# A third query product by an inner Strassen scheme in 128 columns, in a multi-query attention layer

## The chip, the cores and the metric

The kernel runs on one core of a Trainium2 chip. The engines of the core are TensorE (PE, with its weight loads listed apart as PEld), VectorE (DVE), ScalarE (ACT), GpSimd (POOL) and SyncE (SP, which issues the transfers here). The metric is the time of one execution on the device in microseconds; the kernel before takes 1023.08 us, the median of three runs.

## The reference

For each of 64 batches of 128 tokens the layer is attention with 16 query heads and a single key and value head, with a bias, a mask, a null key and a residual:

```python
xn = layernorm(x, g_in)
q = (xn @ Wq).reshape(b, n, H, DH).transpose(0, 2, 1, 3) * scale
kv = xn @ Wkv
k, v = (kv[..., :DH], kv[..., DH:])
...
sim = jnp.einsum('bhid,bjd->bhij', q, k)
...
attn = jax.nn.softmax(sim, axis=-1)
out = jnp.einsum('bhij,bjd->bhid', attn, v)
out = out.transpose(0, 2, 1, 3).reshape(b, n, INNER)
out = out @ Wo
return layernorm(out, g_out)
```

The model width is 512, the inner width 1024 (16 heads of 64), everything in float32. The result is added to x.

## The kernel before, in words

Batches are taken in groups of four (g) for the query product and in pairs (d) for everything else; one pass over a pair is a `turn(d)` (scores and attention times values) followed by a `body(d)` (all else). There is no scheduler: each engine has one queue, and the order in it is the order in which the source lines issue the work. A body of pair d makes, side by side, the key and value product of the next group (`kv_pair`), half of the next group's queries, the softmax of the pair, and the output projection and the norm of the pairs before it.

The query product of a group and the output projection of a pair are each done by Strassen's scheme: seven products of half-size blocks instead of eight. In this text "query product k" is `product(g, f, k)` and "output product k" is `out_product(p, k)`, k from 1 to 7. A query product is made for one chunk f of 128 query columns at a time, with 256 tokens as the moving columns: two matmuls of 128x128 weights and 256 columns, one for each half of the contraction. Each body does two chunks, f0 and f1. An output product is four matmuls of 256 columns.

In the bodies with d > 3 (d = 4 to 29, named `deeper` in the code) query products 2 and 4 are not made as a whole. They are split by Strassen's scheme a second time, into seven single matmuls of 128 columns for both chunks together: `inner_product` and `last_product`. "Inner product k.i" is the i-th of these within query product k. The same scheme is not used there for query product 3.

Partial sums of a scheme accumulate in a PSUM bank, are read out by ScalarE or VectorE, and are accumulated further by the next product: query products 1, 6, 7 of a chunk in bank `a` (`keep` copies the stages p1, u2, u3 to tiles of their own in SBUF), 5 and 3 in bank `c`; output products 1, 6, 7, 4 in bank `X`, 5 and 3 in `Y`. So a product that goes on in a bank must wait until the stage before it has been read. `q_out`, `inner_out`, `last_out` and `out_part` add what stands in PSUM to a kept stage on VectorE. The inner products of query product 4 use the two banks of pool `ps_s`, those of query product 2 one of the two banks of `ps_w`.

On VectorE the same queue holds `scores_max`, `rinv` (reciprocal of the softmax sum), `blocks_T` (a transpose of a batch's whole attention matrix, 128x1536) and the norms' statistics; on POOL it holds `scale` (softmax times the reciprocal), `bias_add`, the token sums of the schemes and the power -0.5 of the norms; ScalarE has the exponentials, the copies of PSUM and the applied norms.

## Time and profile before

| | |
|---|---|
| Time, median of three runs | 1023.08 us (1022.87 to 1023.58) |
| Span of the profiled execution | 1021.2 us |
| Time around the span (median less span) | 1.9 us |
| PE busy | 1012.8 us, 99% |
| PEld busy | 899.6 us, 88% |
| DVE busy | 845.8 us, 83% |
| POOL busy | 769.2 us, 75% |
| ACT busy | 673.1 us, 66% |

Busy time of an engine is the time in which at least one of its instructions is under way. Each float32 matmul of the program is two records in the trace, so one 128x256 matmul is two records of 128x256. The duration in a group of matmuls is that of one record from its start until its result is written; records overlap, so the time that a row of matmuls takes on PE is read from the start of one group to the start of the next. Line numbers are those of the kernel before.

### The profile page before, as it was taken

To read this page: it belongs to the slowest core of one execution; us is meant where nothing else is said; L and a number is where in the kernel's file an instruction comes from. 1 tells how busy PE (TensorE), PEld (TensorE's weight loads), DVE (VectorE), ACT (ScalarE), POOL (GpSimd) and SP (SyncE) were. 2 spreads that over 40 slices of the span, in tenths; PEclk is the share of its full clock that TensorE was granted. 3 is DMA by queue.
4 is the path that set the end of the run, shared out by engine and by line. 5 is a ranking of instruction groups with operands and counts; after the bars stand their busy time and mean duration, and the time that the engine had idled before them with its cause. 6 is when DMAs were issued, how large, how long until landed. Compare 5 with 4: busy or idle time off the path is not lost.

```text
span 1021.2 us, 31459 instructions
## 1 busy us (share of the span) xinstructions
PE 1012.8 (99%) x12333; PEld 899.6 (88%) x12333; DVE 845.8 (83%) x1958; ACT 673.1 (66%) x2753; POOL 769.2 (75%) x633
## 2 busy tenths in 40 slices
PE   9999999999999999999999999999999999999997
PEld 8888888888888888888888888888888888888886
DVE  6777888888888888888888888888898888977787
ACT  5766677656677665686656776566775657865583
POOL 4997768677686877859678696776868768686686
PEclk9999999999999999999999999999999999999999
DMA  7415143151531415225152341514315152140221
GB/s 219 139 30 151 67 122 112 36 154 63 144 98 69 123 56 152 88 74 140 36 152 85 109 120 32 164 63 138 102 50 134 64 152 89 71 111 24 69 85 62
DMA packets 73835, 100.86 MB, mean 99 GB/s; under 512 B 32212, under 2 KB 36056, under 8 KB 71896
## 3 DMA queue, kind: packets, MB, share of 16 engines
q1 hardware_dynamic: 73392, 98.47, 32.5%
q8 instruction: 96, 1.57, 0.6%
q14 instruction: 51, 0.42, 0.1%
q10 hardware_dynamic: 296, 0.40, 0.1%
HBM read 63.19 MB, written 33.55 MB: 95 GB/s over the span
## 4 chain that ended last, share of the span: by engine, by line
PE 96%; POOL 1%; DVE 1%; ACT 1%; issue 0%; DMA 0%; POOLq 0%; DVEq 0%; ACTq 0%
PE pyX L936 20%; PE pa L515 16%; PE pyY L936 10%; PE pc L515 10%; PE po L849 8%; PE pkv L363 6%; PE pyw L936 5%; PE pl L581 4%; PE pm L647 4%; PE ps L718 3%; PE pq L450 3%; PE sc_X L718 2%; PE sc_Y L718 2%; PE sc_a L718 1%; PE py_s L936 1%; ACT s L749 1%
## 5 line engine op out<-in xcount | busy, mean ns | idle before, releaser
L749 ACT ACTIVATE s<-s,nmax 128x65 f32<-128x65 f32 (+1 forms) x1024 | 372.2, 369 | 61.7 <-DVE nmax L740 61.7
L771 POOL TENSOR_TENSOR s<-s,rinv 128x512 f32<-128x512 f32 (+1 forms) x132 | 190.6, 1446 | 133.1 <-DVE rinv L767 133.1
L683 POOL TENSOR_TENSOR s<-biasp,mneg 128x1552 f32<-128x1552 f32 (+1 forms) x65 | 206.2, 3176 | 50.9 <-DVE s L733 26.9
L749 ACT ACTIVATION_READ_ACCUMULATOR s<-s,nmax 128x1 f32 x1024 | 197.1, 192 | 0.0
L787 DVE STREAM_TRANSPOSE sb<-s 128x1536 f32<-128x1536 f32 (+1 forms) x68 | 113.6, 1674 | 11.4 <-POOL s L771 11.4
L740 DVE TENSOR_REDUCE nmax<-s 128x8 f32<-128x1032 f32 (+1 forms) x128 | 121.8, 952 | 0.1
L964 ACT COPY y<-pyX 128x256 f32<-128x256 f32 x29 | 10.8, 372 | 167.5 <-PE pyX L936 129.7
L936 PE MATMUL pyX<-wT,oT 128*128 128x256 f32 x464 | 109.7, 379 | 0.0
L936 PE MATMUL pyX<-wo,oT 128*128 128x256 f32 x464 | 109.7, 379 | 0.0
L936 PEld LDWEIGHTS pyX<-wo,oT 128*128 128x128 f32 x464 | 86.0, 190 | 10.5
L936 PEld LDWEIGHTS pyX<-wT,oT 128*128 128x128 f32 x464 | 84.0, 190 | 9.2
L916 POOL TENSOR_TENSOR oT<-oT 128x512 f32<-128x512 f32 x64 | 80.6, 1277 | 3.9 <-PE pyw L936 1.6
L849 PE MATMUL po<-sb,vr 32*64 32x128 f32 (+1 forms) x3904 | 82.9, 308 | 0.2 <-DVE sb L787 0.2
L527 ACT COPY ku<-pa 128x256 f32<-128x256 f32 x118 | 43.4, 367 | 59.8 <-issue 30.8
L849 PEld LDWEIGHTS po<-sb,vr 32*64 32x64 f32 x3904 | 71.7, 130 | 9.4 <-issue 5.6
L536 DVE TENSOR_TENSOR qT<-pc,ku 128x256 f32<-128x256 f32 x118 | 48.2, 408 | 32.2 <-PE pc L515 19.7
L868 ACT ACTIVATE oT<-po,nv 128x512 f32<-128x512 f32 (+1 forms) x127 | 73.5, 655 | 0.4 <-PE po L849 0.2
L515 PE MATMUL pa<-xS,wq 128*128 128x256 f32 x264 | 67.8, 379 | 0.0
L597 DVE TENSOR_TENSOR qT<-pl,kp 128x128 f32<-128x128 f32 x112 | 32.1, 286 | 42.8 <-PE pl L581 41.9
L281 POOL TENSOR_TENSOR rstd<-rstd,nhalf 128x1 f32<-128x1 f32 x64 | 35.2, 557 | 42.0 <-DVE rstd L280 38.9
L363 PE MATMUL pkv<-xT,wkv 128*128 128x256 f32 x256 | 63.3, 391 | 0.0
L515 PE MATMUL pa<-xT,wq 128*128 128x256 f32 x236 | 60.6, 379 | 0.0
(207 smaller groups left out, 2588.9 us busy)
## 6 DMA issues: line engine op xcount, KB each, us to landing
res<-in_x_dram SPq DMA_DIRECT2D x64, 256.0 KB
out_dram<-y SPq DMA_DIRECT2D x63, 256.0 KB
x<-in_x_dram SPq DMA_DIRECT2D x62, 256.0 KB
xd<-xb SPq DMA_DIRECT2D x14, 1024.0 KB
xT<-xd SPq DMA_DIRECT2D x56, 256.0 KB
vr<-vd SPq DMA_DIRECT2D x64, 128.0 KB
kT<-kT SPq DMA_DIRECT2D x32, 64.0 KB
vd<-vb SPq DMA_DIRECT2D x32, 64.0 KB
```

The costliest lines, as they stand in the source:

```text
L363: nc.tensor.matmul(pkv, wkv[:, kc, :], xT[g][:, t : t + 2, kc, :], start=(kc == 0), stop=(kc == KC - 1),)
L515: nc.tensor.matmul(prod[tag], w[:, kc, f * P : (f + 1) * P], t[:, :, kc, :], start=(start and kc == 0), stop=(kc == HK - 1), skip_group_ch ...
L683: nc.gpsimd.tensor_tensor(S[b][:, :, keys], biasp[:, :, keys], mneg[:, t, keys] .unsqueeze(1) .broadcast_to([P, R8, keys.stop - keys.start ...
L718: nc.tensor.matmul(home[r][u * DH : (u + 1) * DH, f, :], qT[g, f, t // 2][rows, t % 2, hf, u], kT[rows, 0 : nk // Q, t, :], start=True, st ...
L740: nc.vector.tensor_reduce(nmax[b][:, hf], S[b][:, :, WITH_NULL[hf]], AX.X, ALU.max, negate=True)
L749: nc.scalar.activation(row, row, AF.Exp, bias=nmax[b][:, hf, k : k + 1], accum_out=rsum[b][:, hf, k : k + 1],)
L771: nc.gpsimd.tensor_tensor(sv, sv, rinvs[b, hf][:, lo:hi].unsqueeze(2).broadcast_to([P, hi - lo, sv.shape[2]]), ALU.mult,)
L787: nc.vector.transpose(sbs[b][:, :, lo:hi].rearrange("p j e q -> p e j q"), S[b][:, lo:hi, 1 : ROW - 1].rearrange("p e (j k) -> p e j k", k=Q),
L849: nc.tensor.matmul(po[s][rows, to : to + n], vr[g][quad, t, PLACE[j], :], sb[quad, slots, r * NF : (r + 1) * NF, :], start=(turn == 0), st ...
L868: nc.scalar.activation(to, src, AF.Identity, bias=nv2)
L916: eng.tensor_tensor(o, a, b, op)
L936: nc.tensor.matmul(prod[key], h[:, c, :], w[:, c, :], start=(start and c == 0), stop=(c == HC - 1), skip_group_check=not start,)
```

## The change

**Query product 3** of the bodies with d > 3 is made by the second scheme as well: seven matmuls of 128 columns for both chunks (`inner_products(3, ...)`) take the place of two products of two 256-column matmuls each. Inner products 3.2, 3.3 and 3.4 accumulate into bank `c` on top of query product 5; 3.1, 3.5, 3.6 and 3.7 go to one of the two banks of `ps_s`, whose other bank holds the inner products of query product 4. Both banks are one tile, `pi34`.

**Both chunks' chain in one bank.** `product_two` makes query products 1, 6, 7 and 5 for f0 and f1 one after the other into the two halves of a bank, `keep_two` and `q_out_two` read both halves with one instruction of 512 columns.

**Partial sums** are no longer kept in tiles of their own, but in the query and output tiles in which the result will stand (`KEPT`, `Y_KEPT`).

**Norms in pairs.** `two_stats` and `two_nmr` do the small operations of a norm for two batches with one instruction each; the statistics of the output norm stand at the start of a body instead of one half at the end of the body before.

**The bodies** with d > 3 are a new function, `body_full`, with an order of its own.

```diff
+    def two_stats(tiles, name):
+        mv = small.tile([P, 2, 2], FP, tag=f"mv{name}", name=f"mv{name}")
+        rstd = small.tile([P, 2], FP, tag=f"rs{name}", name=f"rs{name}")
+        sts = []
+        for t in tiles:
+            st = small.tile([P, 6], FP, tag="st", name="st")
+            nc.vector.bn_stats(st, t)
+            sts.append(st)
+        for i, st in enumerate(sts):
+            nc.vector.bn_aggr(mv[:, i], st)
+        nc.vector.tensor_scalar(rstd, mv[:, :, 1], EPS, None, ALU.add)
+        nc.gpsimd.tensor_tensor(rstd, rstd, nhalf.broadcast_to([P, 2]), ALU.pow)
+        return mv, rstd
+    def two_nmr(mv, rstd, name):
+        nmr = small.tile([P, 2], FP, tag=f"nm{name}", name=f"nm{name}")
+        nc.vector.scalar_tensor_tensor(
+            nmr, mv[:, :, 0], -1.0, rstd, ALU.mult, ALU.mult
+        )
+        return [(nmr[:, i : i + 1], rstd[:, i : i + 1]) for i in range(2)]
...
-    def keep(tag, name, slot=None):
...
+    KEPT = {"p1": (0, 0), "u2": (0, 1), "u3": (HC, 0)}
+    def keep(tag, g, f, name):
+        u, h = KEPT[name]
+        nc.scalar.copy(
+            q_part(g, u + f, h), prod[tag].rearrange("p (t h i) -> p t h i", t=2, h=2)
+        )
...
+    def product_two(g, j, k, pool, tag, start=True):
+        if start:
...
+        w, t = operands(g, k)
+        for i in range(2):
+            f = 2 * j + i
+            for kc in range(HK):
+                first = start and i == 0 and kc == 0
+                nc.tensor.matmul(
+                    prod[tag][:, i],
+                    w[:, kc, f * P : (f + 1) * P],
+                    t[:, :, kc, :],
+                    start=first,
+                    stop=(kc == HK - 1),
+                    skip_group_check=not (start and i == 0),
...
+    def keep_two(tag, g, j, name):
+        u, h = KEPT[name]
+        nc.scalar.copy(
+            q_whole(g, j, u // HC, h).rearrange("p f t h i -> p (f t h) i"),
+            prod[tag].rearrange("p f (n i) -> p (f n) i", i=DH),
+        )
+    def q_out_two(g, j, u, h, tag, name):
+        v, k = KEPT[name]
+        nc.vector.tensor_tensor(
+            q_whole(g, j, u, h).rearrange("p f t h i -> p (f t h) i"),
+            prod[tag].rearrange("p f (n i) -> p (f n) i", i=DH),
+            q_whole(g, j, v // HC, k).rearrange("p f t h i -> p (f t h) i"),
+            ALU.add,
+        )
...
-    def inner_product(g, h, k):
...
-    def last_product(g, h, k):
...
+    def token_sums_inner(g, k):
+        b = {
+            2: xT[g][:, 0 : GB // 2, hi_k],
+            3: xT[g][:, GB // 2 :, hi_k],
+            4: xS.get((g, 4)),
...
+        for o, p, m in (*sums, (t2, b22, t1), (t4, b21, t2)):
+            nc.gpsimd.tensor_tensor(o, p, m, ALU.subtract)
+    A2, A1, A0 = range(3)
+    def inner_room(k, g, h):
+        if k == 2:
+            inner[k] = ps_w.tile([P, 4, N], FP, tag="w", name=f"pi2_{g}_{h}")
+        else:
+            two = ps_s.tile([P, 2, 4, N], FP, tag="s", name=f"pi34_{g}_{h}")
+            inner[3], inner[4] = two[:, 0], two[:, 1]
+    def inner_products(k, g, h, which):
+        for i in which:
+            if k == 3 and i in (2, 3, 4):
+                n = {2: 0, 3: 1, 4: 2}[i]
+                to = prod["c"].rearrange("p f (t n) -> p (f t) n", t=2)[:, n]
+            else:
+                at = {1: A0, 2: A2, 3: A1, 4: A0, 5: A1, 6: A0, 7: A0}[i]
+                to = inner[k][:, at]
+            nc.tensor.matmul(
+                to,
+                inner_w[k][i][:, h],
+                inner_x[k, g][i],
+                start=(i == 1),
+                stop=True,
+                skip_group_check=(i != 1),
+            )
+    def inner_out(k, g, h, part):
+        u, hh = DEST[k]
+        q = q_whole(g, h, u, hh)
+        r = inner[k].rearrange("p a (h i) -> p a h i", h=2)
+        four = q.rearrange("p f t h i -> p (f t) h i")
+        o, p = {
...
+            "00,11": (four[:, 0:4:3], r[:, A2 : A1 + 1]),
...
+            "01,10": (four[:, 1:3], r[:, A1 : A0 + 1]),
+            "1*": (q[:, 1], r[:, A0 : A0 + 1].broadcast_to([P, 2, 2, DH])),
+            "*1": (q[:, :, 1], r[:, A1 : A1 + 1].broadcast_to([P, 2, 2, DH])),
+        }[part]
+        nc.vector.tensor_tensor(o, p, o, ALU.add)
...
-    def out_keep(tag, name, slot):
...
+    Y_KEPT = {"yp1": (0, 0), "yu2": (0, 1), "yp5": (1, 1)}
...
+    def body_full(d):
...
+        on = two_stats((ys[l], ys[l + 1]), "o")
+        if sums:
+            token_sums_inner(g, 2)
+            token_sum(g, 3)
...
+        nmrs[l], nmrs[l + 1] = two_nmr(*on, "o")
+        if xw:
+            xn = two_stats((xs[m], xs[m + 1]), "x")
+        scores_max(a, 1)
+        product_two(g, h, 1, ps_q, "a")
+        keep_two("a", g, h, "p1")
+        pair_norm(l)
+        inner_room(2, g, h)
+        inner_products(2, g, h, (1,))
+        inner_out(2, g, h, "00")
...
+        out_product(p, 1, ps_y, "X")
+        out_keep(p, "X", "yp1")
...
+        product_two(g, h, 6, ps_q, "a", start=False)
+        keep_two("a", g, h, "u2")
...
+        product_two(g, h, 5, ps_q, "c")
...
+        inner_products(2, g, h, (6,))
+        inner_out(2, g, h, "01")
+        out_product(p, 2, ps_w, "w")
+        out_part(p, 0, "w")
...
+        exps(a, 1, 0, 4)
+        product_two(g, h, 7, ps_q, "a", start=False)
+        keep_two("a", g, h, "u3")
+        inner_products(2, g, h, (7, 5, 2))
+        inner_out(2, g, h, "11")
+        inner_out(2, g, h, "00,11")
+        if sums:
+            token_sums_inner(g, 3)
+            token_sums_inner(g, 4)
+        inner_room(4, g, h)
+        inner_products(3, g, h, (1,))
+        q_out_two(g, h, 1, 1, "c", "u3")
+        inner_out(3, g, h, "00")
+        out_product(p, 5, ps_y, "Y")
+        exps(a, 1, 4)
+        rinv(a, 1)
+        scale(a, 1)
+        scale(b, 0)
+        out_keep(p, "Y", "yp5")
+        inner_products(3, g, h, (6, 5))
+        inner_out(3, g, h, "01")
+        inner_products(2, g, h, (4, 3))
+        inner_out(2, g, h, "01,10")
+        inner_products(4, g, h, (1,))
+        inner_out(4, g, h, "00")
+        exps(b, 1, 0, 3)
+        out_product(p, 6, ps_y, "X", start=False)
+        out_keep(p, "X", "yu2")
+        inner_products(3, g, h, (7,))
+        exps(b, 1, 3)
+        blocks_T(a)
+        rinv(b, 1)
+        scale(b, 1)
+        bias_add(b + 2)
+        inner_out(3, g, h, "1*")
+        inner_out(3, g, h, "*1")
+        inner_products(4, g, h, (6,))
+        inner_out(4, g, h, "01")
+        inner_products(3, g, h, (2, 3, 4))
+        q_out_two(g, h, 0, 1, "c", "u2")
+        out_product(p, 3, ps_y, "Y", start=False)
+        out_part(p, 1, "Y")
+        inner_products(4, g, h, (7, 5, 2))
+        inner_out(4, g, h, "11")
+        inner_out(4, g, h, "00,11")
+        out_product(p, 7, ps_y, "X", start=False)
+        out_part(p + 1, 1, "X")
+        inner_products(4, g, h, (4, 3))
+        inner_out(4, g, h, "01,10")
+        blocks_T(b)
+        out_product(p, 4, ps_y, "X", start=False)
+        out_part(p + 1, 0, "X", False)
...
-        body(d)
+        (body_full if d > 3 else body)(d)
```

The order on the engines at three places of body d = 15 (group 8, second half). Names: `pa`, `pc`, `pyX`, `pyY`, `pl`, `pm`, `pi2`, `pi34` are PSUM tiles (banks a, c, X, Y; inner products of query product 2 before, of 4 before, of 2 now, of 3 and 4 now), `qT` queries, `sb` the transposed attention, `y` the output rows.

PE from output product 6 to output product 3, or the inner product behind it, before:

```order
L647 MATMUL pm_8_1_6906<-xM_8_6461,wM_92 128x128 x2
L936 MATMUL pyX_28_1_6828<-wT_140,oT_28_6752 128x256 [waits Pool_49]
L936 MATMUL pyX_28_1_6828<-wT_140,oT_28_6752 128x256 x3
L515 MATMUL pa_8_3_1_6878<-xS3_8_6368,wq_81 128x256 [waits Activation_49]
L515 MATMUL pa_8_3_1_6878<-xS3_8_6368,wq_81 128x256
L647 MATMUL pm_8_1_6906<-xS4_8_6419,wq_81 128x128 [waits DVE_49]
L936 MATMUL pyY_28_5_6933<-wo_90,oT_28_6752 128x256 [waits Pool_49]
L936 MATMUL pyY_28_5_6933<-wo_90,oT_28_6752 128x256 x3
```

and now:

```order
L982 MATMUL pyX_28_1_6468<-wT_141,oT_28_6400 128x256 [waits Pool_49]
L982 MATMUL pyX_28_1_6468<-wT_141,oT_28_6400 128x256 x3
L681 MATMUL pi34_8_1_6543<-xI3_8_6153,wS_138 128x128 [waits DVE_49]
L681 MATMUL pi34_8_1_6543<-xI4_8_6157,wM_92 128x128 [waits DVE_49]
L681 MATMUL pc_8_1_5_6488<-xT_8_5732,wS_138 128x128
L681 MATMUL pc_8_1_5_6488<-xT_8_5732,wN_140 128x128
L681 MATMUL pc_8_1_5_6488<-xI3_8_6153,wS_138 128x128
L982 MATMUL pyY_28_5_6547<-wo_90,oT_28_6400 128x256 [waits Activation_49,Pool_49]
L982 MATMUL pyY_28_5_6547<-wo_90,oT_28_6400 128x256 x3
L681 MATMUL pi34_8_1_6543<-xS4_8_6082,wq_81 128x128 [waits DVE_49]
```

Query product 7 and an inner product of query product 4 stood between output products 6 and 3. Now 3.7, 4.6, 3.2, 3.3 and 3.4 stand there, and 4.7, 4.5 and 4.2 behind output product 3. 4.6 is the row of `pi34` with `xI4` and `wM`. It has a wait for VectorE, and the count that it waits for is the one that the row of 128x2x2x64 among the VectorE rows below reaches.

VectorE at the same place, before (from the inner sum behind which the transpose stands):

```order
L663 TENSOR_TENSOR qT_8_2_0_6757<-pm_8_1_6906,ku3_6855 128x2x64 [waits PE_49]
L787 STREAM_TRANSPOSE sb_30_6960<-s_30_6323 128x8x6x32 [waits Pool_49]
L948 COPY kyu2_6966<-pyX_28_1_6828 128x256 [waits PE_49]
L767 RECIPROCAL rinv_31_1_6968<-rsum_31_6822 128x8 [waits Activation_49]
L536 TENSOR_TENSOR qT_8_3_1_6760<-pc_8_3_5_6940,ku3_6973 128x4x64 [waits Activation_49]
L663 TENSOR_TENSOR qT_8_3_0_6759<-pm_8_1_6906,ku3_6973 128x2x64 [waits PE_49]
L663 TENSOR_TENSOR qT_8_3_0_6759<-pm_8_1_6906,qT_8_3_0_6759 128x2x64 [waits DVE_49]
L966 TENSOR_TENSOR y_28_6864<-pyY_28_5_6933,kyu2_6966 128x256 [waits PE_49]
```

and now:

```order
L1009 COPY y_28_6473<-pyX_28_1_6468 128x256 [waits PE_49]
L833 STREAM_TRANSPOSE sb_30_6594<-s_30_5994 128x8x6x32 [waits Pool_49]
L813 RECIPROCAL rinv_31_1_6596<-rsum_31_6458 128x8 [waits Activation_49]
L709 TENSOR_TENSOR qT_8_1_1_6406<-pi34_8_1_6543,qT_8_1_1_6406 128x4x64 [waits PE_49]
L709 TENSOR_TENSOR qT_8_1_1_6406<-pi34_8_1_6543,qT_8_1_1_6406 128x2x2x64 [waits DVE_49]
L709 TENSOR_TENSOR qT_8_1_0_6405<-pi34_8_1_6543,qT_8_1_0_6405 128x2x64 [waits PE_49]
L605 TENSOR_TENSOR qT_8_1_1_6406<-pc_8_1_5_6488,qT_8_1_1_6406 128x8x64 [waits DVE_49,PE_49]
```

The copy of output product 6 stood behind the transpose and stands ahead of it; behind the transpose and the reciprocal now stand the two sums that read 3.7 and 3.5 (`"1*"` and `"*1"`), and then the sum that reads 4.6 (`"01"`).

PE at the end of the body, from output product 7 to output product 4, before:

```order
L936 MATMUL pyX_28_1_6828<-wo_90,oT_28_6752 128x256 [waits DVE_49]
L936 MATMUL pyX_28_1_6828<-wo_90,oT_28_6752 128x256 x3
L515 MATMUL pc_8_3_5_6940<-xT_8_6054,wS_138 128x256 [waits DVE_49]
L515 MATMUL pc_8_3_5_6940<-xT_8_6054,wS_138 128x256
L647 MATMUL pm_8_1_6906<-xS4_8_6419,wR_93 128x128 [waits DVE_49]
L647 MATMUL pm_8_1_6906<-xM_8_6461,wq_81 128x128
L936 MATMUL pyX_28_1_6828<-wT_140,oT_28_6752 128x256 [waits DVE_49]
L936 MATMUL pyX_28_1_6828<-wT_140,oT_28_6752 128x256 x3
```

and now:

```order
L681 MATMUL pi34_8_1_6543<-xS4_8_6082,wq_81 128x128
L982 MATMUL pyX_28_1_6468<-wo_90,oT_28_6400 128x256 x4
L681 MATMUL pi34_8_1_6543<-xI4_8_6157,wq_81 128x128 [waits DVE_49]
L681 MATMUL pi34_8_1_6543<-xS4_8_6082,wR_93 128x128
L982 MATMUL pyX_28_1_6468<-wT_141,oT_28_6400 128x256 [waits DVE_49]
L982 MATMUL pyX_28_1_6468<-wT_141,oT_28_6400 128x256 x3
```

Query product 3 of chunk f1 and two inner products stood between output products 7 and 4, both in bank X; now two inner products, 4.4 and 4.3, stand there.

More of the change, by code (lines that the diff above doesn't have):

```diff
@@ L1093, in body_first @@
         g, m = 1, 2 * GB
[L1094 removed]
+        q_next(g, 0)
         pkv = kv_pair(g * GB)
@@ L1419, in body @@
             store(l + 1)
+        norm_apply(m + 1)
+        exps(a, 1, 0, 1)
+        product(g, f0, 4, ps_q, "a", start=False)
+        q_out(g, HC + f0, 0, "a")
+        product(g, f0, 3, ps_q, "c", start=False)
+        q_out(g, f0, 1, "c", "u2")
+        tokens_T(m)
+        tokens_T(m + 1)
+        if h == 1:
+            tokens_out(g + 1)
+            tokens_in(g + 1)
+        for r in (p, p + 1):
+            load_res(r)
+        load_x(m + 2)
+        load_x(m + 3)
+        exps(a, 1, 1, 4)
@@ new lines, in body @@
+        exps(b, 1, 0, 2)
+        if h == 1:
+            values_T(g)
+        product(g, f1, 5, ps_q, "c")
+        out_product(p, 5, ps_y, "Y")
+        out_keep(p, "Y", "yp5")
+        exps(b, 1, 2, 3)
+        product(g, f1, 6, ps_q, "a", start=False)
+        keep("a", g, f1, "u2")
+        if deep:
+            inner_products(2, g, h, (4, 3))
[4 more added lines that the diff above has]
+        out_keep(p, "X", "yu2")
```

593 lines of the change are left out of this document (241 added, 352 removed).

## The prediction

> **What bounds the kernel now.** I read the page first, then stretches of two bodies each, then the order in time of one body. From the page, and one of the stretches (length, then busy time of PE, PEld, DVE, ACT, POOL):
>
> ```profile
> span 1021.2 us, 31459 instructions
> PE 1012.8 (99%) x12333; PEld 899.6 (88%) x12333; DVE 845.8 (83%) x1958; ACT 673.1 (66%) x2753; POOL 769.2 (75%) x633
> ...
> 435.40:497.60 62.20, 62.20 (x779) 55.43 (x773) 52.77 (x126) 41.65 (x171) 46.95 (x39) 1.00 0.34 100
> ```
>
> PE is busy in every microsecond of a pair of bodies. So PE's own work counts in full, and so does every wait that the change puts in front of it; the other engines count only by these waits. Body d = 15 on PE, in order of time (start, length, instructions), and one group of a second-scheme sum, which comes four times in a body with d > 3:
>
> ```profile
> 501.96 0.30 PEld L363 LDWEIGHTS pkv<-xT,wkv 128*128 128x128 f32 x2 [0.17 <-DVE s L733]
> ...
> 501.96 1.99 PE L363 MATMUL pkv<-xT,wkv 128*128 128x256 f32 x8
> 503.80 1.03 PE L515 MATMUL pa<-xT,wq 128*128 128x256 f32 x4
> ...
> 512.46 1.03 PE L515 MATMUL pc<-xT,wS 128*128 128x256 f32 x4
> 513.32 0.61 PE L647 MATMUL pm<-xS,wq 128*128 128x128 f32 x4
> 513.77 0.39 PE L581 MATMUL pl<-xL,wq 128*128 128x128 f32 x2
> ...
> 518.34 1.89 PE L936 MATMUL pyX<-wT,oT 128*128 128x256 f32 x8
> 520.07 1.03 PE L515 MATMUL pa<-xS,wq 128*128 128x256 f32 x4
> ...
> 522.88 1.89 PE L936 MATMUL pyX<-wo,oT 128*128 128x256 f32 x8
> 524.61 1.03 PE L515 MATMUL pc<-xT,wS 128*128 128x256 f32 x4
> 525.47 0.38 PE L647 MATMUL pm<-xS,wR 128*128 128x128 f32 x2
> 525.69 0.39 PE L647 MATMUL pm<-xM,wq 128*128 128x128 f32 x2
> 525.91 1.89 PE L936 MATMUL pyX<-wT,oT 128*128 128x256 f32 x8
> L663 DVE TENSOR_TENSOR qT<-pm,ku 128x128 f32<-128x128 f32 x104 | 29.1, 280 | 0.5
> ```
>
> From start to start: a query product of one chunk 0.86 us (512.46 to 513.32), an inner product 0.225 (0.45 for two), an output product 1.73 (518.34 to 520.07). 104 / 4 = 26 bodies get the new order; all sums below are for one of them, times 26.
>
> **What it removes and adds on PE.** Out: query product 3 of two chunks, 1.72 us. In: seven inner products, 7 x 0.225 = 1.57. Saving 0.15 to 0.19 (0.22 for one at 525.47); I take 0.17, so 4.4 us in all.
>
> **What it moves.** The loops that decide are those in which PE writes into a bank, another engine reads it, and PE may go on only then. Their prices, on VectorE and PE, from two neighbouring bodies, and the one loop that is bare in this trace, at the very end (output product 7, the sum, output product 4, in one bank):
>
> ```profile
> 490.07 1.89 PE L936 MATMUL pyY<-wo,oT 128*128 128x256 f32 x8
> 491.80 1.89 PE L936 MATMUL pyX<-wo,oT 128*128 128x256 f32 x8
> ...
> 490.38 0.39 DVE L948 COPY kyu<-pyX 128x256 f32<-128x256 f32 x1
> 490.69 0.18 DVE L767 RECIPROCAL rinv<-rsum 128x8 f32<-128x8 f32 x1
> 490.80 0.37 DVE L536 TENSOR_TENSOR qT<-pc,ku 128x256 f32<-128x256 f32 x1
> ...
> 492.00 0.42 DVE L966 TENSOR_TENSOR y<-pyY,kyu 128x256 f32<-128x256 f32 x1 [0.31 <-PE pyY L936]
> ...
> 515.58 0.28 DVE L597 TENSOR_TENSOR qT<-pl,kp 128x128 f32<-128x128 f32 x1
> 515.89 0.29 DVE L597 TENSOR_TENSOR qT<-pl,qT 128x128 f32<-128x128 f32 x1
> ...
> 518.75 1.77 DVE L787 STREAM_TRANSPOSE sb<-s 128x1536 f32<-128x1536 f32 x1
> 520.43 0.39 DVE L948 COPY kyu<-pyX 128x256 f32<-128x256 f32 x1
> ...
> 1011.24 1.89 PE L936 MATMUL pyc<-wo,oT 128*128 128x256 f32 x8
> 1013.71 1.99 PE L936 MATMUL pyc<-wT,oT 128*128 128x256 f32 x8 [0.57 <-DVE y L966]
> ...
> 1013.23 0.42 DVE L966 TENSOR_TENSOR y<-pyc,kyp 128x256 f32<-128x256 f32 x1 [0.47 <-PE pyc L936]
> ```
>
> VectorE starts 0.20 us after PE has issued its last matmul (491.80 to 492.00). PE goes on 0.06 us after VectorE's end (1013.65 to 1013.71). After such a wait (the 0.17 in the row at 501.96) PE loses another 0.10: its first eight records take 1.84 (501.96 to 503.80) instead of 1.73. The bare loop took 1013.71 - (1011.24 + 1.73) = 0.74.
>
> *Inner product 4.6.* It stands one inner product (3.7) behind output product 6, and its wait is for the second of the two sums `"1*"`, `"*1"`, though these read 3.7 and 3.5, in the other bank of the same tile. On VectorE, counted from the end of issue of output product 6, stand ahead: start of the copy 0.20, copy 0.31 (490.38 to 490.69), transpose 1.68 (518.75 to 520.43), reciprocal 0.11 (490.69 to 490.80), the first sum 0.45 (128x256 takes 0.42, and a sum on the same tile starts 0.03 after the end, 515.89 against 515.58 + 0.28), the second 0.42: 3.17, and PE goes on at 3.23. It has 0.22 of work until then. So PE waits 3.01 + 0.10 = 3.11. Behind it on PE's queue is all the rest of the body; VectorE has nothing to do with this wait, it is itself at work. Inner product 4.7 then waits for the sum of 4.6, which output product 3 and three inner products hide.
>
> *Inner product 4.1* waits in the same way for the sum of 3.6 (`"01"`), which VectorE starts when 3.5 is done: 0.20 + 0.29 + 0.06 = 0.55, less the 0.45 of inner products 2.4 and 2.3: 0.10 + 0.10 = 0.20.
>
> *Output product 4* goes on in bank X when the sum of output product 7 has read it: the bare loop, 0.74. Before, 1.30 us of other products covered it (524.61 to 525.91); now 4.4 and 4.3 do, 0.45: 0.29 + 0.10 = 0.39.
>
> Sum: 3.11 + 0.20 + 0.39 - 0.17 = 3.53 us a body, 91.8 in all.
>
> **What costs nothing.** Whether the transpose itself is held up depends on `scale` of a's second half, on POOL, and the reciprocal on the exponentials of b:
>
> ```profile
> 486.74 1.91 POOL L771 TENSOR_TENSOR s<-s,rinv 128x1024 f32<-128x1024 f32 x1
> ...
> 519.81 0.19 ACT L749 ACTIVATION_READ_ACCUMULATOR s<-s,nmax 128x1 f32 x1
> ...
> L868 ACT ACTIVATE oT<-po,nv 128x512 f32<-128x512 f32 x116 | 69.2, 673 | 0.2 <-issue 0.2
> L281 POOL TENSOR_TENSOR rstd<-rstd,nhalf 128x1 f32<-128x1 f32 x64 | 35.2, 557 | 42.0 <-DVE rstd L280 38.9
> L560 POOL TENSOR_TENSOR xL<-xT 128x256 f32<-128x256 f32 x14 | 10.2, 728 | 0.0
> L562 POOL TENSOR_TENSOR xL<-xT,xL 128x128 f32<-128x128 f32 x14 | 6.4, 456 | 1.1
> ```
>
> In the fuller body (d even, with the token sums) `scale` ends at 488.65, 0.84 us ahead of the transpose's new start (output product 6 ends there at 490.07 - 1.08 = 488.99; plus 0.51 is 489.50). The sums for query product 3 add 0.73 + 2 x 0.46 = 1.64 ahead of it, two of four powers go (1.11 less), and b's first `scale` stands behind it now, so it comes no later; if a power of two columns takes twice one, 0.7 later, still in time. The exponentials of b end some 0.8 us after output product 6 and the reciprocal comes 2.2 after it. The copies of 512 columns (0.67) in place of two of 256 leave the loop in bank `a` at 0.20 + 0.67 + 0.06 = 0.93 against 1.95 of products 2.1 and output 1 between; query products 5 and output 2 cover the next by more. VectorE's fewer small instructions and sums of 256 and 512 columns are off the path: if VectorE were late all through the body, each 0.1 us of it ahead of `"*1"` would cost 2.6 us in all. The statistics that moved to the body's start are needed by an applied norm that stands behind a copy which is itself 1.2 us later. The three bodies with d < 4 keep their order on PE. Keeping partial sums in the result's tiles adds no instruction.
>
> **The clock.** A wait of 3 us is new for this kernel. At the end of the trace PE stops at 1015.70 (1013.71 + 1.99); at its start it is slow:
>
> ```profile
> 1015.00:1016.00 1.00, 0.70 (x4) 0.27 (x2) 0.80 (x2) 0.00 (x0) 0.17 (x1) 1.00 0.67 262
> ...
> 1018.00:1019.00 1.00, 0.00 (x0) 0.00 (x0) 0.45 (x2) 0.00 (x0) 0.00 (x0) 0.73 0.05 19
> ...
> 1.35 3.35 PE L1556 MATMUL busy<-wR 128*128 128x128 f32 x14 [1.35 <-POOL neg L245]
> ...
> 9.01 5.52 PE L450 MATMUL pq<-xT,wq 128*128 128x128 f32 x48
> ```
>
> The third number from the end is the granted clock: 0.73 in the microsecond from 1018, that is 1.00 until 1018.46 and 0.50 from then on, 2.76 us after PE's last result. In the new wait PE writes nothing from 0.38 to 3.23, 2.85 us: just longer. A record of 128 columns took 0.24 us at the start (3.35 / 14) and 0.115 later (5.52 / 48): half speed for some 3.4 us. A fall costs half of that, 1.7. Between none and 26 falls I take 9, a third, since 2.85 lies so near to the one delay seen: 15.3 us. [...]
>
> Sum: 1021.2 + 91.8 + 15.3 = 1128.3 of span, and with the 1.9 us between this span and the median of 1023.08: 1130.
>
> **Rivals.**
> - *The clock holds*: 1021.2 + 91.8 + 1.9 = 1115. For it: no wait in the trace has shown a fall inside the kernel; against: the 2.76.
> - *The clock falls in every body*: 26 x 1.7 = 44, 1159.
> - *4.6 waits only for what it overwrites*, the sum of 4.1, long done. Then 4.7 is the one that waits, for `"01"`, 3.17 - 0.08 + 0.29 + 0.06 = 3.44 against 2.84 of PE's work: 0.60 + 0.10. 26 x (0.70 + 0.20 + 0.39 - 0.17) = 29, 1052. Against it: the wait stands at 4.6's row, by its count.
> - *Faster*: VectorE gets through copy, transpose, reciprocal and two sums in the 0.22 us that 3.7 takes, and the last loop hides as well: only the 4.4 remain, 1018.7. It decides from a chain on VectorE under 0.3 us, where a transpose alone takes 1.68.
>
> **The numbers.** Some falls of the clock 45%, none 30%, all 15%, the wait by what is overwritten 5%, longer waits than computed (VectorE or POOL late, over 1162) 2%, no change within 0.2% (2 us, about what a measurement of this kernel can tell) 1%, faster 2%. Slower is 97%. The range: with no fall and the shortest steps (4.6 at 2.9, 4.1 at nothing, output product 4 at 0.24, saving 0.19: 2.95 a body) 1100; with a fall in every body 1159 and some lateness: 1162.
>
> **What would show it.** PE's busy share falls to about 92%. In a body PE should stand idle once for 3.0 us ahead of an inner product into `pi34` with `xI4` and `wM`, put down to the VectorE sum into `qT`; 0.2 and 0.4 us twice more; a period of two bodies of 69 to 72 us instead of 62.2. The granted clock of stretches below 1.00 shows the falls. If 4.6 starts at once after 3.7, the wait is not what I read in it; if the stretches read 62, the whole chain is wrong.

## The result, and the profile after

The changed kernel takes 1142.85 us (median of six runs) against 1023.14 us before. The ratio, 1.1158 with a 95% interval of 1.1135 to 1.1181, is that of the five fast runs (1137.97 to 1146.43 us); the sixth, at 1164.91 us, was slow. The profiled execution has a span of 1144.5 us, 123.3 more than before. From its page: span, busy time of the engines, and the granted clock of PE in 40 slices.

```profile
span 1144.5 us, 31441 instructions
PE 1056.8 (92%) x12489; PEld 926.0 (81%) x12489; DVE 881.9 (77%) x1794; ACT 673.2 (59%) x2675; POOL 774.4 (68%) x621
...
PEclk9999999999899999999989999999999889999999
```

PE's busy share fell from 99% to 92%, and the row of the clock, 9 in every slice before, has dips to 8. The list of waits (engine and line that waits, who is waited for: us in total, times, longest) shows one large wait of PE, once in each of the 26 bodies with d > 3, and a small one of its weight loads:

```profile
PE pi L681 <- DVE qT L709: 75.9, 26, 2.9
...
PEld pyX L982 <- DVE y L1016: 6.8, 26, 0.3
```

Body d = 16, in which the clock held, on PE in order of time (start, length, instructions, wait ahead), from one `kv_pair` to the next:

```profile
591.35 1.99 PE L388 MATMUL pkv<-xT,wkv 128*128 128x256 f32 x8
...
607.29 0.39 PE L681 MATMUL pi<-xT,wL 128*128 128x128 f32 x2
607.62 0.49 PE L681 MATMUL pi<-xS,wq 128*128 128x128 f32 x2
607.94 1.89 PE L982 MATMUL pyX<-wT,oT 128*128 128x256 f32 x8
609.67 0.38 PE L681 MATMUL pi<-xI,wS 128*128 128x128 f32 x2
612.96 0.46 PE L681 MATMUL pi<-xI,wM 128*128 128x128 f32 x2 [2.90 <-DVE qT L709]
613.25 0.39 PE L681 MATMUL pc<-xT,wS 128*128 128x128 f32 x2
...
618.27 0.39 PE L681 MATMUL pi<-xS,wR 128*128 128x128 f32 x2
618.73 1.99 PE L982 MATMUL pyX<-wT,oT 128*128 128x256 f32 x8
620.65 0.27 PE L764 MATMUL sc_Y<-kT,qT 64*64 64x64 f32 x2
...
625.97 1.35 PE L388 MATMUL pkv<-xT,wkv 128*128 128x256 f32 x5
```

and VectorE beside the long wait, which is at work the whole time:

```profile
609.87 0.42 DVE L1009 COPY y<-pyX 128x256 f32<-128x256 f32 x1 [1.44 <-PE pyX L982]
610.21 1.77 DVE L833 STREAM_TRANSPOSE sb<-s 128x1536 f32<-128x1536 f32 x1
611.90 0.16 DVE L813 RECIPROCAL rinv<-rsum 128x8 f32<-128x8 f32 x1
611.99 0.83 DVE L709 TENSOR_TENSOR qT<-pi,qT 128x256 f32<-128x256 f32 x2
```

The three waits stand where the change put them. Ahead of inner product 4.6 (612.96) PE is idle for 2.90 us, from the last result of 3.7 until the two sums of query product 3 have ended; counted from start to start, 4.6 begins 612.96 - (609.67 + 0.22) = 3.07 late. 4.1 (607.62) starts 0.11 late, 618.73 (output product 4) 0.24 late, and each is followed by a slow start of some 0.10 (607.62 to 607.94 is 0.32 instead of 0.22; 618.73 to 620.65 is 1.92 instead of 1.82 before); behind 4.6 it is 0.07 (612.96 to 613.25). The body takes 625.97 - 591.35 = 34.62 us, 3.54 more than the same one before (31.08); other bodies with d even whose clock held take 3.53 more. Those with d odd take 3.58 more; there the wait is 2.94.

In other bodies the clock falls. Stretches of 2 us in body d = 6 (length, then busy time of PE, PEld, DVE, ACT, POOL; the third number from the end is the granted clock), and PE's rows there:

```profile
249.00:251.00 2.00, 0.06 (x1) 0.00 (x0) 2.00 (x4) 0.28 (x2) 0.81 (x1) 1.00 0.26 100
251.00:253.00 2.00, 1.04 (x9) 1.07 (x10) 1.07 (x4) 0.00 (x0) 1.85 (x1) 1.00 0.16 62
253.00:255.00 2.00, 2.00 (x7) 1.62 (x7) 0.69 (x1) 0.00 (x0) 2.00 (x2) 0.60 0.02 4
255.00:257.00 2.00, 2.00 (x10) 1.79 (x8) 0.42 (x1) 0.00 (x0) 1.21 (x1) 0.55 0.00 0
257.00:259.00 2.00, 2.00 (x13) 1.79 (x12) 0.79 (x3) 0.00 (x0) 0.00 (x0) 1.00 0.00 0
```

```profile
251.96 0.46 PE L681 MATMUL pi<-xI,wM 128*128 128x128 f32 x2 [2.90 <-DVE qT L709]
...
252.93 3.16 PE L982 MATMUL pyY<-wo,oT 128*128 128x256 f32 x8
255.88 0.64 PE L681 MATMUL pi<-xS,wq 128*128 128x128 f32 x2
```

The wait ends at 251.96 with the clock still full; it falls to 0.50 at 253.4, 1.4 us *after* PE has begun to work again, and output product 3 takes 255.88 - 252.93 = 2.95 us instead of 1.73. The trace's record of the clock has 12 such falls, eight of 3.41 us and four of 6.83, 54.6 us at half speed, of which 3.2 lie in the waits themselves; half of the other 51.4 is lost, 25.7 us. The sum of the profiled execution: 26 bodies at 3.53 or 3.58 are 92.4; the clock 25.7; 5.2 remain of the 123.3.

### The profile page after: what moved, and what is told of

Same layout as the page of the kernel before. It is cut to its first block, busy times and chain, and to the rows that moved or that the text cites. A ratio compares the mean times of both kernels' runs of the same rounds, so it can differ in the third digit from the quotient of the medians.

```text
span 1144.5 us, 31441 instructions
## 1 busy us (share of the span) xinstructions
PE 1056.8 (92%) x12489; PEld 926.0 (81%) x12489; DVE 881.9 (77%) x1794; ACT 673.2 (59%) x2675; POOL 774.4 (68%) x621
## 4 chain that ended last, share of the span: by engine, by line
PE 86%; DVE 9%; POOL 2%; DMA 1%; issue 1%; ACT 1%; SPq 0%; POOLq 0%; DVEq 0%
PE pyX L982 18%; PE pa L587 12%; PE pyY L982 11%; PE pi L681 9%; PE po L895 7%; PE pkv L388 5%; PE pyw L982 4%; DVE sb L833 4%; PE pc L587 4%; PE ps L764 2%; PE pa L538 2%; PE sc_X L764 2%; PE pc L681 2%; DVE qT L709 2%; PE sc_Y L764 2%
## 5 line engine op out<-in xcount | busy, mean ns | idle before, releaser
L795 ACT ACTIVATION_READ_ACCUMULATOR s<-s,nmax 128x1 f32 x1024 | 194.1, 190 | 0.0
L709 DVE TENSOR_TENSOR qT<-pi,qT 128x128 f32<-128x128 f32 (+1 forms) x376 | 128.2, 342 | 57.0 <-PE pi L681 50.3
L982 PE MATMUL pyX<-wT,oT 128*128 128x256 f32 x464 | 112.4, 385 | 1.9
L681 PE MATMUL pi<-xI,wM 128*128 128x128 f32 x104 | 25.2, 328 | 75.9 <-DVE qT L709 75.9
L895 PE MATMUL po<-sb,vr 32*64 32x128 f32 (+1 forms) x3904 | 86.7, 308 | 1.6 <-issue 1.2
L681 PEld LDWEIGHTS pi<-xI,wM 128*128 128x128 f32 x104 | 18.6, 224 | 80.5 <-DVE qT L709 40.7
L982 PE MATMUL pyY<-wo,oT 128*128 128x256 f32 x256 | 78.6, 463 | 0.0
L982 PEld LDWEIGHTS pyY<-wo,oT 128*128 128x128 f32 x256 | 57.7, 234 | 9.3
L982 PE MATMUL pyw<-wo,oT 128*128 128x256 f32 x256 | 60.5, 379 | 0.0
```

Source lines behind the costliest of these rows:

```text
L681: nc.tensor.matmul(to, inner_w[k][i][:, h], inner_x[k, g][i], start=(i == 1), stop=True, skip_group_check=(i != 1),)
L709: nc.vector.tensor_tensor(o, p, o, ALU.add)
L795: nc.scalar.activation(row, row, AF.Exp, bias=nmax[b][:, hf, k : k + 1], accum_out=rsum[b][:, hf, k : k + 1],)
L895: nc.tensor.matmul(po[s][rows, to : to + n], vr[g][quad, t, PLACE[j], :], sb[quad, slots, r * NF : (r + 1) * NF, :], start=(turn == 0), st ...
L982: nc.tensor.matmul(prod[key], h[:, c, :], w[:, c, :], start=(start and c == 0), stop=(c == HC - 1), skip_group_check=not start,)
```

## The experiments

Times are medians, beside the kernel before on the same chip (1023.04 to 1023.35). "Change" is the changed kernel.

**e1: the inner products of query product 4 in a tile of their own.** The order stays.

```diff
-            two = ps_s.tile([P, 2, 4, N], FP, tag="s", name=f"pi34_{g}_{h}")
-            inner[3], inner[4] = two[:, 0], two[:, 1]
+            inner[3] = ps_s.tile([P, 2, 4, N], FP, tag="s", name=f"pi3_{g}_{h}")[:, 0]
...
+        inner[4] = ps_w.tile([P, 4, N], FP, tag="w", name=f"pi4_{g}_{h}")
         inner_products(4, g, h, (1,))
```

> The inner products of query product 4 get a tile of their own, in the pool that also holds those of query product 2, instead of the second half of pi34; no order is changed. Theory (4.6 waits for the sums of query product 3 only because both halves are one tile): the 2.9 us wait ahead of 4.6 is gone; 4.7 is the next that waits, for its own sum "01" behind the transpose, 3.50 us after output product 6 against 2.85 us of work on PE, 0.65 + 0.10; 4.1 no longer waits for a sum of query product 3. A body then costs 0.75 + 0.39 - 0.17 = 0.97 us more than before, 25 us in all: about 1048 us, clock 1.00 throughout. Rival (4.6 truly needs what VectorE does there, or VectorE is late as a whole): the wait stays in front of 4.6, 1115 us or more.

Measured: 1050.88 us, ratio 1.0276 (1.026 to 1.0291). The same place on PE, 4.6 to 4.7:

```profile
565.02 0.39 PE L680 MATMUL pi<-xI,wM 128*128 128x128 f32 x2
...
565.91 1.89 PE L981 MATMUL pyY<-wo,oT 128*128 128x256 f32 x8
568.20 0.49 PE L680 MATMUL pi<-xS,wq 128*128 128x128 f32 x2 [0.39 <-DVE qT L708]
```

4.6 (565.02) starts without a wait. 4.7 (568.20) starts 568.20 - (565.91 + 1.73) = 0.56 late, since its own sum stands behind the transpose; the row puts 0.39 of it down to the wait. So most of the long wait was for sums that 4.6 does not need, through the shared tile. Undisturbed bodies cost 0.84 and 0.96 more than before, as reckoned (0.97).

**e2: the two sums ahead of the transpose on VectorE.** Only VectorE's order changes.

```diff
+        inner_out(3, g, h, "1*")
+        inner_out(3, g, h, "*1")
         blocks_T(a)
         rinv(b, 1)
...
-        inner_out(3, g, h, "1*")
-        inner_out(3, g, h, "*1")
```

> Only VectorE's order is changed: the two sums of 3.7 and 3.5 stand ahead of the transpose and the reciprocal instead of behind them. Theory (4.6 waits for the whole chain on VectorE, and the transpose is 1.7 us of it): copy to 0.51, two sums to 1.38, PE goes on at 1.44 us after output product 6, a wait of 1.22 + 0.10 instead of 3.11; the waits ahead of 4.1 and of output product 4 stay. 26 x (1.32 + 0.20 + 0.39 - 0.17) = 45 us over before: about 1068 us. The clock stays at 1.00, since idle times of 1.2 us lie under the 1.96 us that the trace of the changed kernel shows ahead of its falls. Rival (the wait is for something else that comes just as late, POOL or the exponentials): the wait stays near 2.9 us and the time near 1143.

Measured: 1074.31 us, ratio 1.05 (1.0484 to 1.0516).

```profile
575.58 0.38 PE L681 MATMUL pi<-xI,wS 128*128 128x128 f32 x2
577.14 0.46 PE L681 MATMUL pi<-xI,wM 128*128 128x128 f32 x2 [1.18 <-DVE qT L709]
```

The wait shrank from 2.90 to 1.18 us, by the transpose and the reciprocal, and the clock never fell (mean 0.999). It is the chain on VectorE that PE waits for, link by link. A body costs 1.81 or 1.85 more than before (1.74 expected); 26 of them are 47.6 of the 51.5 us that the span is longer.

**e3: the wait filled with work that nobody needs.**

```diff
         inner_products(3, g, h, (7,))
+        idle = ps_w.tile([P, HE], FP, tag="w", name=f"idle_{p}")
+        for i in range(6):
+            nc.tensor.matmul(
+                idle, oT[p][:, 0, 0, :], e11[:, 0, :], start=True, stop=True
+            )
```

> The changed kernel with six matmuls of 256 columns between 3.7 and 4.6, whose result nobody reads (2.6 us of PE's work in the place where it waits for 3). The chain on VectorE is not touched, so the bodies should not get shorter by themselves. Theory (some 27 us of the loss are the clock, which falls because PE is idle): granted clock 1.00 throughout, and 26 x 3.53 = 92 us over before, 1115 us. Rival (the clock has nothing to do with this wait, or the low clock costs nothing that the wait does not hide): the time stays at 1138 to 1147.

Measured: 1120.15 us, ratio 1.0949 (1.0932 to 1.0965). PE there, and span and clock of the core:

```profile
596.99 2.76 PE L1612 MATMUL idle<-wo,oT 128*128 128x256 f32 x12
600.05 0.46 PE L681 MATMUL pi<-xI,wM 128*128 128x128 f32 x2 [0.31 <-DVE qT L709]
```

```profile
core 0: 1118.8 us, clock 1.000
```

The bodies are as long as in the change (3.53 or 3.57 more where nothing disturbs them), but the clock stays full and 1144.5 - 1118.8 = 25.7 us of span are gone, as many as the record of the clock gave. Doing useless work there is faster than waiting: this part of the loss is the clock's, and PE's idle time brings it. The time lies 5 us over the 1115 expected; what most of them are, e4 and e10 tell.

**e8: the wait 1 us longer**, by half of the transpose made twice.

```diff
         blocks_T(a)
+        nc.vector.transpose(
+            sbs[a][:, :, 0 : R8 // 2].rearrange("p j e q -> p e j q"),
+            S[a][:, 0 : R8 // 2, 1 : ROW - 1].rearrange("p e (j k) -> p e j k", k=Q),
+        )
```

> The changed kernel with half of the transpose made twice: the chain on VectorE, and with it the wait ahead of 4.6, gets some 0.85 us longer (2.92 to 3.77). Theory (the clock falls when one of a row of fixed stretches of 3.41 us holds about 1.96 us or more of PE's idle time): 3.77 us cannot be split over two stretches without one of them holding nearly that much, so the clock falls in 25 or 26 of 26 bodies instead of in 12. Wait 26 x 0.85 = 22 us more, clock some 60 us instead of 27: about 1198 us (1185 to 1215). Rival (falls come by chance, or by the length of the wait only beyond some other limit): about as many falls as now, 12 to 15, and 1165 to 1172 us.

Measured: 1192.66 us, ratio 1.1656 (1.1637 to 1.1676).

```profile
PE pi L681 <- DVE qT L709: 102.3, 26, 4.0
```

The wait is 3.93 us on average and the record has 26 falls in 26 bodies, 92.2 us at half speed, 2.8 of them in the waits, so 44.7 us lost: 26 x (3.55 + 1.01) + 44.7 = 163.3 of the 169.1 us that the span is longer. The number of falls is as forecast; each costs 1.72 us, since only one took two stretches of 3.41 us, where in the change four of 12 did.

**e4: the body reordered, all work kept.** Both sets of inner products go in step, and 3.2 to 3.4 move between output products 7 and 4.

```diff
         inner_products(3, g, h, (1,))
+        inner_products(4, g, h, (1,))
...
         out_product(p, 5, ps_y, "Y")
...
+        inner_products(2, g, h, (4, 3))
         inner_products(3, g, h, (6, 5))
+        inner_products(4, g, h, (6,))
...
         out_product(p, 6, ps_y, "X", start=False)
...
         inner_products(3, g, h, (7,))
+        inner_products(4, g, h, (7, 5, 2))
...
         out_product(p, 3, ps_y, "Y", start=False)
...
         out_product(p, 7, ps_y, "X", start=False)
...
+        inner_products(3, g, h, (2, 3, 4))
         inner_products(4, g, h, (4, 3))
...
         out_product(p, 4, ps_y, "X", start=False)
```

> The changed kernel with its body reordered, all work kept. The inner products of query products 3 and 4 go in step, so that no product into pi34 stands right behind a sum that reads it: 3.1 and 4.1 ahead of output product 5; 2.4, 2.3, 3.6, 3.5 and 4.6 behind it; output product 6; 3.7, 4.7, 4.5 and 4.2; output products 3 and 7; 3.2, 3.3, 3.4, 4.4 and 4.3 between output products 7 and 4. Theory (the whole loss is three loops without cover and the clock behind one of them; the saving on PE is real): each loop now has 1.1 to 5 us of other products over it, PE is at 99%, and only the 0.17 us a body that the seven inner products save remain: 1023.0 - 4.4 = 1018.7 us. Rival (the new body costs something besides: larger copies, sums in pairs, POOL's powers, DVE's queue): at 1023 or above.

Measured: 1023.66 us, ratio 1.0005 (0.9996 to 1.0013): all of the loss is gone, but the gain is not there. Of the 25 bodies that are followed by another, 16 are 0.10 to 0.17 us shorter than before, most by 0.16, so the saving is real. Others are up to 0.54 longer. Of the five that are over 0.1 longer four lose it in the same place, attention times values (`po`) between bodies, and the fifth in the key and value product right behind it. PE's `po` at two places of this kernel and at one before:

```profile
530.63 3.24 PE L895 MATMUL po<-sb,vr 32*64 32x256 f32 x124
...
562.25 2.55 PE L895 MATMUL po<-sb,vr 32*64 32x256 f32 x120
```

```profile
530.58 2.63 PE L849 MATMUL po<-sb,vr 32*64 32x256 f32 x124
```

The same 124 records take 3.24 us instead of 2.63. The list of waits has more "issue" ahead of `po` than before, which is time in which PE waited for nothing that the profile shows (before, and then e4):

```profile
PEld po L849 <- issue: 5.6, 32, 0.3
```

```profile
PEld po L895 <- issue: 7.9, 37, 0.5
```

**e5, e6, e7: three parts of it one by one,** all against e4. e5 puts 3.2 to 3.4 back ahead of output product 3; e6 does the small operations of the norms one batch at a time; e7 makes query product 3 as a whole.

```diff
+        inner_products(3, g, h, (2, 3, 4))
+        q_out_two(g, h, 0, 1, "c", "u2")
         out_product(p, 3, ps_y, "Y", start=False)
...
-        inner_products(3, g, h, (2, 3, 4))
-        q_out_two(g, h, 0, 1, "c", "u2")
```

> As the reordered body, but 3.2, 3.3 and 3.4 stand ahead of output product 3 again, so that only 4.4 and 4.3 (0.45 us) lie between output products 7 and 4, as in the changed kernel. Theory: the loop of 0.74 us in bank X comes through with 0.29, and 0.10 for the start after it: 0.39 x 26 = 10.1 us more than the reordered body, about 1028.8 us. Rival (that loop is hidden or was not part of the loss): no difference to the reordered body.

e5: 1031.81 us, 8.2 more than e4. The small wait of the weight loads for the sum in bank X is back, as in the change (6.8 us, 26 times), and its 0.24 and the slow start of 0.10 are 8.8 for 26 bodies; 10.1 were expected from 0.29.

```diff
-        nc.vector.tensor_scalar(rstd, mv[:, :, 1], EPS, None, ALU.add)
-        nc.gpsimd.tensor_tensor(rstd, rstd, nhalf.broadcast_to([P, 2]), ALU.pow)
+            r = rstd[:, i : i + 1]
+            nc.vector.tensor_scalar(r, mv[:, i, 1:2], EPS, None, ALU.add)
+            nc.gpsimd.tensor_tensor(r, r, nhalf, ALU.pow)
```

> As the reordered body, but the small operations of the norms are done for one batch at a time again (addition, power, product: two instructions each instead of one of two columns), at the same places. Theory (the norms in pairs lie off the path, on VectorE and POOL, and are worth nothing while PE is the bound): as the reordered body within 0.5 us, 1018.7. Rival (the pairs relieve VectorE's or POOL's queue ahead of something that PE waits for): 1 us or more above it.

e6: 1027.83 us, 4.2 more: the expectation failed. PE now waits for POOL's token sums:

```profile
PE pi L688 <- POOL xI L668: 0.9, 5, 0.2
```

```profile
PEld pi L688 <- POOL xI L668: 3.0, 9, 0.4
```

The loss lies mostly in bodies with d even, where those sums are made (eight of 13 are 0.29 to 0.42 longer than before, the undisturbed ones with d odd 0.16 shorter). In this order the norms in pairs are worth something, since POOL's queue reaches the sums earlier.

```diff
-        inner_products(3, g, h, (2, 3, 4))
+        product_two(g, h, 3, ps_q, "c", start=False)
```

> As the reordered body, but query product 3 is not split: two chunks of two matmuls of 256 columns, into bank c between output products 7 and 4, and none of its sums on VectorE. It isolates what the split itself is worth on PE. Theory: 1.72 us in place of 7 x 0.225 = 1.57 us, 0.17 x 26 = 4.4 us more than the reordered body, 1023.1. Rival (the split is worth nothing on PE, since short products cost more than half of long ones): the same as the reordered body.

In e7 one quarter of the weights of query product 3 holds the differences of the split scheme, so its queries are not the reference's; the work is that of the whole product. 1034.22 us, 10.6 more than e4 and not 4.4. Bodies with d odd take as long as before (0.00 in most, against -0.16 in e4), which is the split's worth as reckoned. Those with d even take 0.65 more: without 3.5 and 3.6 ahead of it, 4.6 comes to POOL's token sums too early (3.8 us of waits for them on PE, 6.0 on its weight loads). One body also loses 1.5 us, 1.4 of it in a wait for a transfer. So e7 measured more than one thing; only the odd bodies answer its question.

**e10 and e9: the number of instructions.** What was odd in e4 are the transfers that load instructions. Its page has 98 of them on one queue, 16 KB each:

```profile
q8 instruction: 98, 1.61, 0.6%
```

PE and PEld have 24978 instructions there: an estimate of some 255 for each, if that queue is theirs. From the records of the transfers: when loads start, counted from the start of a body (less than zero is ahead of it), beside the time from the first `po` to that start.

```
before  d = 9..12   po 2.47 2.48 2.47 2.48   loads -6.0 -1.7 2.6 | -6.0 -1.5 2.0 | -6.5 -1.7 2.6 | -5.8 -1.9 1.9
e4      d = 8..11   po 2.94 2.47 2.48 2.47   loads -9.2 -3.0 0.9 19.4 | -2.8 0.6 18.6 | -3.2 0.4 19.1 | -3.2 0.3 17.2
e4      d = 15..16  po 3.07 3.17             loads -3.7 -0.1 14.8 | -3.9 -0.2 10.0
e10     d = 27..28  po 3.39 4.12             loads -7.7 -2.7 0.9 | -7.7 -3.3 7.2 20.0
e9      d = 9..12   po 2.63 2.56 2.56 2.56   loads -6.6 -1.9 1.8 | -5.0 -1.6 1.9 | -6.5 -1.9 1.8 | -5.5 -1.3 2.1
```

Before, a body has 760 or 768 instructions on PE in the trace, weight loads included (a float32 matmul is four); that is what three loads of some 255 hold, and in most bodies they stand at nearly the same places. The seven matmuls in place of four add twelve instructions, and the loads drift. e10 is the kernel *before*, with the same work in more instructions (776 a body), and e9 is e4 brought back to 756 or 764:

```diff
-        values(p, WIDE if 4 < d < PAIRS - 1 else ())
-        values(p + 1, WIDE if 4 < d < PAIRS - 1 and (d % 2 or d % 10 == 4) else ())
+        values(p)
+        values(p + 1)
```

> The kernel before, with none of the small products of attention and values merged: the same columns, the same order, but 780 to 782 instructions on PE in a body instead of 763 to 772. Theory (the loads of PE's instructions drift): most bodies as before, some 0.1 to 0.7 us longer in attention times values, in groups of neighbouring bodies where a load falls into it, 4 to 5 us in all: about 1027.5 us. Rival (the number of instructions has no effect, or a merged matmul is itself cheaper): no difference, or the same small difference in every body.

```diff
+        values(p, (1, 3) if 4 < d < PAIRS - 1 else ())
+        values(
+            p + 1,
+            () if not 4 < d < PAIRS - 1 else (1, 3) if d % 10 in (4, 9) else WIDE,
+        )
```

> As the reordered body, with more of the small products of attention and values merged in pairs (the second and third step of a row group as one matmul of twice the columns, for two of the four row groups instead of one, at most): the columns that PE works through stay the same, but a body has about 768 instructions on PE (counted in the program, with weight loads) instead of 779 to 785. The trace of the reordered body shows that the time missing there is lost in attention times values, 2.47 us in most bodies and up to 3.17 in some, where the loads of PE's instructions (three of 16 KB a body, seen among the transfers) come at another place of the body each time, while before they stand at the same three places in every body. Theory (a program whose bodies are not a whole number of such loads long lets them drift into the stretch that uses instructions fastest): 2.47 us in every body, and the 4.4 us of the saving appear: 1018.7 us. Rival (the losses have to do with VectorE's or POOL's new order, not with the number of instructions): near 1023.7 as the reordered body.

e10: 1029.53 us, ratio 1.0063 (1.005 to 1.0077). Twelve of its 25 bodies are as before within 0.05, others longer by up to 1.65, in groups. One of them:

```profile
908.71 2.47 PE L849 MATMUL po<-sb,vr 32*64 32x256 f32 x122
912.47 0.44 PE L849 MATMUL po<-sb,vr 32*64 32x128 f32 x6 [1.28 <-issue]
912.84 1.99 PE L363 MATMUL pkv<-xT,wkv 128*128 128x256 f32 x8
```

PE stops for 1.28 us in the middle of `po`, waiting for no other engine. So more instructions for the same work are enough to bring the loss. That a load falls into `po`, as the expectation had it, is not what costs: before, one starts there, 0.8 to 2.1 us ahead of the body, in every body with d > 3. What the stops have in common the traces show. From one start on PE to the next, the bodies with d > 3 of e4 and e10 have eleven stops of over 0.3 us that the kernel before does not have, nine in `po` and two in the key and value product right behind it. Each ends 1.3 to 1.6 us after a load has ended, and within a run they stand a whole number of times some 254 instructions apart, close to the estimate of 255 for a load. By these counts PE stands at the border between two loads. e9: 1022.77 us, ratio 0.9993 (0.9985 to 1.0002). Its loads stay in place in most bodies, no such stop is left, and "issue" ahead of `po` is back to the 5.6 us of before,

```profile
PEld po L895 <- issue: 5.6, 32, 0.3
```

but `po` takes 2.56 us (2.63 in every fifth body) instead of 2.47. The merging costs 0.09 a body, 2.3 us, half of the saving. The rivals, new orders on VectorE or POOL as the cause of e4's lost gain, fall with e10, which has neither, and with e9, which has both and no stops.

**e11: the merged step elsewhere,** to get those 0.09 back.

```diff
+                if s == 1 and s in wide and turn > 1:
+                    if turn == 3:
+                        continue
+                    j, to, n = 2, 1, 1
```

> As the reordered body with the even number of instructions, but a row group whose second and third step are merged does its last step one place earlier where it is the second of the four, so that in each step three or four row groups have work and not two. In the run without it the loads of PE's instructions stand at the same three places in every body, as meant, but attention times values takes 2.56 us in every body instead of 2.47. Theory (the 0.09 come from the step in which only two of the four row groups work): 2.47 us again, 26 x 0.09 = 2.3 us less than that run, about 1020.4 us, 0.3% under the kernel before. Rival (the 0.09 belong to the merged matmul itself): no difference, 1022.8 us.

Measured: 1022.86 us, ratio 0.9995 (0.9986 to 1.0004), and `po` at 2.56 us still in most bodies. The theory of the step with two row groups falls; why the merged products cost more is open. So no version was measurably faster than the kernel before.

## Why the prediction was right, point by point

The direction, the mechanism and the range (1100 to 1162) held; 1130 was 13 us too low. In the profiled execution (1146.43 us) the span is 1144.5 against 1128.3 forecast: 10.4 more for the clock, 5.2 that were in no term, 0.6 in the waits.

- **PE bounds the kernel, so each wait counts in full.** Right. In bodies whose clock held, the four terms (3.11 + 0.20 + 0.39 - 0.17 = 3.53) came to 3.53 and 3.58. One by one, counted as the prediction counts, from start to start: the wait of 4.6 was put at 3.01 and is 3.07 to 3.10; that of 4.1 at 0.10, and is 0.11; that of output product 4 at 0.29, and is 0.24; a slow start at 0.10, and is 0.07 to 0.10; the saving at 0.17, and is 0.16 (e4, e7). The small misses cancel, so the agreement to the hundredth is luck, though each term is right to within 0.1.
- **4.6 waits for sums that it does not need.** Right: with a tile of its own (e1) the wait is gone, and the next in line is 4.7, as the rival with the narrower wait had it. That rival gave 1052 us, and e1, which makes it true, took 1051. So close is luck: the 0.20 of 4.1 is gone in e1, its undisturbed bodies cost 0.84 to 0.96 and not 1.12, and 4.3 us that were in no term make up for it.
- **The transpose is over half of the chain.** Right (e2: 1.72 us less wait with the transpose and the short reciprocal out of the chain).
- **The clock.** The mechanism was right (e3), the size was not: 9 of 26 falls at 1.7 us, 15.3 us, were 12 falls and 25.7 us in the profiled execution. The 9 was a guess, and the 12 belong to one execution: its mean granted clock is 0.976, and in other executions of the same kernel it was up to 0.982. The step that failed was to read the fall at the end of the trace as a delay of 2.76 us after PE's last result, and to let chance decide how often 2.85 reaches it. In the trace of the change the falls go with how a wait lies across stretches of 3.413 us (below), and four of the falls took two such stretches, so that a fall cost 2.14 us on average and not 1.7.
- **The rest, 5.2 us, was not in the sum.** The prediction counted PE's work by its duration and never its instructions. What remains beside the undisturbed bodies and the clock is 4.3 us in e1, 3.9 in e2, 5.3 in e3, 5.8 in e8 and 4.5 in e4 (span over before, less 26 undisturbed bodies and the clock): about the same in every run with some twelve more instructions a body (e3 has 36), whatever its waits. In e10, which adds only instructions, it is 6.8. Most of it stands in `po` of the bodies with d > 3: some 4 us in the change, 2.8 to 5.5 in the other five and 6.1 in e10. Some 0.4 to 1.0 us stand ahead of these bodies; in the change PE waits there once, in the body d = 2, for a sum on VectorE, though its order on PE is unchanged.
- **What was put at nothing.** For larger copies, partial sums in the result's tiles and VectorE's sums e4 shows this: PE waits for none of them. For the norms in pairs no run shows it in the change as it stands; where the waits are gone, the pairs are worth 4.2 us (e6).
- **Faster** (1018.7 us) stays out of reach even with all three waits covered: e4 came to 1023.66 and e9 to 1022.77.

## What to carry to other kernels

Two results that are read and written in turn should not share a tile: in the change a write into one half waited 2.90 us for the readers of the other, and these for the copy, the transpose (1.77 us) and the reciprocal ahead of them on VectorE; with a tile of its own that wait was gone (e1). Where one engine bounds, put the loops of two schemes in step, so that every write has other products between it and the reading that it waits for (1142.85 us in the change, 1023.66 in e4). And count instructions as well as time: this loop, with 760 or 768 instructions a body before, lost 4.5 us with twelve short ones more, and their work saves 26 x 0.16 = 4.2 (e4).

## What the runs showed of the hardware

- **The record of the clock lies on a grid.** In the change it changes only on a grid of 3.413 us. Laying PE's idle times of the change over it, all 12 falls follow a stretch with 1.97 us of idle time or more, and the 14 bodies without one have 2.00 or less in any stretch; in e8 all 26 falls follow one with 2.03 or more. At half speed, a stretch with 0.72 to 0.93 us of idle time was followed by a second one at half speed (four times in the change), while at full speed stretches with up to 2.00 were followed by full speed. Of the 26 waits of 2.9 us, 12 brought a fall and 14 did not, by where they lay; those of 1.2 (e2) never did.
- **PE stops that go with loads of instructions.** They came in and right behind attention times values, where some 250 instructions go by in 2.47 us: up to 1.65 us lost in one body, 6.8 us of span in e10 as a whole. The eleven stops of e4 and e10 end 1.3 to 1.6 us after the end of a load of 16 KB; further on in these bodies, where the 16 instructions of an output product take 1.73 us, there is none. Why there is a stop in one body and none in the next was not tested.
